# The last three attention units written out one by one, router columns cast later, eight zero products first

## The chip, the cores and the metric

The kernel runs on one core of one Trainium2 chip. The metric is the device time of one execution in microseconds. Its engines work side by side, each in the order of its own queue: TensorE (PE; its weight loads are PEld), VectorE (DVE), ScalarE (ACT), GpSimd (POOL) and SyncE (SP), which issues most DMAs.

## What is computed

A cross-attention layer and a mixture-of-experts layer, each with a layer norm ahead and a residual. Sizes: 32 sequences of 100 tokens (3,200 tokens), width 512, 16 heads of 32, 16 experts of 1,024 hidden units, all in float32.

```
q = (layernorm(x) @ WQ.T), k = ctx[:, :100] @ WK.T, v = ctx[:, :100] @ WV.T    # causal, so 100 keys are enough
x = x + softmax(mask(q k.T / sqrt(32))) v @ Wfc.T + bfc
h = layernorm(x)
shared = (gelu(h @ Ws_g.T) * (h @ Ws_u.T)) @ Ws_d.T
scores = softmax(h @ gate_w.T)              # over 16 experts
for each expert: its 12 best tokens of each sequence (384 tokens), gated MLP, times the score
out = x + shared + sum of the experts' parts, added back at the tokens' rows
```

The context has 722 rows for a sequence; the causal mask leaves the first 100.

## The kernel before

Each float32 operand of a large product is split into a high part (a cast on ACT, type fp32r) and a low part (a subtraction, source minus high part), and a product is three products, high by high, high by low, low by high (`mm3`, line 55). "A split" below is such a cast and subtraction.

**Attention** walks 32 units: eight blocks of four sequences (400 tokens) times four chunks of four heads. `prologue()` (L309) loads and splits the projection weights and the first context blocks, and computes the first keys and values. Keys and values go to DRAM (`kD`, `vD`) and come back by `kload` and `vload`. Then the loop over `u` works on three units at a time, in an order written out by hand:

- unit u: its query projection `qproj` on PE and `qkeep` on ACT; the key and value projections of a later context block, while there are any
- unit u-1: `scores` on PE into PSUM tile `sc` (one buffer of four banks); `sm_max` on DVE (16 small operations with the mask and the row maximum), `sm_sub` on POOL, `sm_exp` on ACT, `sm_sum` on DVE (sum and reciprocal), `sm_mul` on POOL, in two halves of two sequences
- unit u-2: `p_turn` (four transposes on PE into PSUM tile `ms`, two buffers), `p_keep` (copied out by ACT), `values` on PE (also into `ms`)
- unit u-3: `y_keep`, ACT's copy of the values, and their store to `yD`

Every engine's queue has exactly this order: PE, ACT, DVE and SP are under a manual schedule in the whole kernel, POOL in the attention. An instruction that waits holds everything behind it on its engine.

**Preparation of the first token group.** The FFN works on groups of two or three tiles of 128 tokens. For group 0 (three tiles) the loop's last three units also carry the steps of class `Prep`: `load_y`, `load_x`; `split_y(i)` (ACT and DVE), `bias(i)` (POOL, or DVE), `fc(i)` (twelve products on PE into `kv`, two buffers), `add(i)`, `stats(i)` (DVE), `rsqrt(i)` (POOL), `norm(i)` (DVE), `store(i)` (a DMA), `turn(i)` (four transposes on PE into `ms`, then a split), `logits` and `tokens` (the router's columns). In the loop they hang on `end`, which is 0, 1, 2 in units 29, 30, 31. After the loop follows a tail for unit 31's softmax and values, within which `F.begin` issues the first `gate_up_mm` of the FFN on PE and `F.begun` its gelu.

**Weight chunks.** The shared expert's and the experts' weights come as chunks of 128 x 1536 (eight to an expert, 768 KB). `chunk_load` issues the DMA of the next chunk into one of two raw buffers; `chunk_split(n, part)` splits it, whole or a third at a time, and then asks for the next load, which waits until the raw buffer is free.

**Router columns.** `load_consts` (L571), called in unit 13, issues three loads (bias, row bases, router weights `gr`), clears `gw` on POOL, and splits `gr` into `gw` at once (L577 on ACT, L578 on DVE).

The order inside unit 31 (`end == 2`) before, as an example, with the lines of other cases left out:

```
                if end == 2:
                    pr.add(2)
                    pr.stats(2)
                    pr.rsqrt(1)
                    pr.store(0)
...
                if end == 2:
                    pr.norm(1)
```

## Time and profile before

| | |
|---|---|
| median of 3 runs | 1696.91 us (1696.52 to 1699.1) |
| the profiled execution's own time | 1700.42 us |
| its span, first to last instruction | 1698.3 us |
| mean granted TensorE clock | 0.991 |
| attention with the preparation | 0 to about 389 us of the span |
| busy: PE, PEld, DVE, ACT, POOL | 98%, 90%, 55%, 41%, 36% |

Every line of a timeline has the start in us, the duration in us, engine, source line, operation, output <- input, and in brackets the time for which the engine was idle just before it and what released it. In a list of waits the numbers are the total, the number of waits and the longest. "Granted clock" is the share of TensorE's full clock in that stretch. Idle time of an engine costs something only where PE ends up waiting for it.

### The profile page before, as it was taken

What the parts mean: (1) busy time and instruction counts of PE and PEld (TensorE: products, weight loads), DVE (VectorE), ACT (ScalarE), POOL (GpSimd) and SP (SyncE); (2) the same over time, 40 slices, a digit from 0 to 9 for tenths busy, and PEclk for the clock granted to TensorE, in tenths of its full rate; (3) what the DMA queues carried; (4) which work ended last, traced back from release to release, by engine and by line L of the source; (5) the groups of instructions that cost most, each with busy time, mean ns of one, the idle gap of its engine ahead of it and who ended that gap; (6) DMA issues with size and microseconds to landing.
All of it is one profiled execution on the core that took longest, in us unless ns stands there. A gap on an engine that the chain in (4) does not pass through costs nothing.

```text
span 1698.3 us, 27985 instructions
## 1 busy us (share of the span) xinstructions
PE 1668.4 (98%) x10838; PEld 1533.6 (90%) x10838; DVE 929.2 (55%) x2191; ACT 691.0 (41%) x1097; POOL 619.5 (36%) x534
## 2 busy tenths in 40 slices
PE   7999999989999999999999999999999999999999
PEld 6998899879999999989899999999999999999998
DVE  4777677685434344344555555555555555555542
ACT  4555555543222112122334444444444444444442
POOL 3877777661110111110143443433444333344011
PEclk9999999999999999999999999999999999999999
DMA  6445444434322123210445554555554555555452
GB/s 211 151 141 160 134 135 121 160 113 143 104 75 70 52 71 97 82 57 27 147 153 160 156 163 152 147 160 160 166 159 145 162 150 152 163 168 152 133 168 63
DMA packets 97892, 224.35 MB, mean 132 GB/s; under 512 B 13633, under 2 KB 49186, under 8 KB 97760
## 3 DMA queue, kind: packets, MB, share of 16 engines
q1 hardware_dynamic: 84528, 197.08, 35.7%
q0 software_dynamic: 12944, 25.22, 7.9%
q8 instruction: 85, 1.39, 0.3%
q14 instruction: 47, 0.39, 0.1%
q10 hardware_dynamic: 288, 0.27, 0.0%
HBM read 175.34 MB, written 47.18 MB: 131 GB/s over the span
## 4 chain that ended last, share of the span: by engine, by line
PE 93%; DVE 2%; ACT 1%; POOL 1%; DMA 1%; issue 1%; SPq 0%; ACTq 0%; POOLq 0%; DVEq 0%
PE gu L55 48%; PE dn L55 24%; PE kv L55 11%; PE m L55 3%; PE ms L280 2%; PE sc L239 2%; PE ms L295 2%; POOL p L259 1%; DVE p L250 1%; PE m L989 1%; ACT pt L285 1%; PE ms L170 0%; DMA kD<-kk 0%; DMA big<-yD 0%; ACT p L263 0%
## 5 line engine op out<-in xcount | busy, mean ns | idle before, releaser
L55 PE MATMUL gu<-xh,whl 128*128 128x384 f32 (+1 forms) x3200 | 645.4, 333 | 0.0
L55 PEld LDWEIGHTS gu<-xh,whl 128*128 128x128 f32 x3200 | 560.6, 188 | 17.2 <-issue 0.3
L638 DVE TENSOR_TENSOR whl<-wraw,whl 128x1536 fp32r<-128x1536 f32 (+1 forms) x146 | 256.6, 1758 | 206.3 <-ACT whl L637 184.7
L55 PE MATMUL dn<-whl,hh 128*128 128x512 f32 x1168 | 368.0, 396 | 0.0
L840 POOL DMA_INDIRECT gx<-xnD,iq x180 | 226.7, 1259 | 362.2 <-DVE big L871 301.9
L55 PE MATMUL gu<-xl,whl 128*128 128x384 f32 (+1 forms) x1600 | 337.8, 332 | 0.0
L55 PEld LDWEIGHTS gu<-xl,whl 128*128 128x128 f32 x1600 | 280.7, 188 | 0.0
L673 ACT CAST hh<-g 128x384 fp32r<-128x384 f32 (+1 forms) x200 | 100.9, 505 | 409.0 <-DVE g L670 380.6
L55 PEld LDWEIGHTS dn<-whl,hh 128*128 128x128 f32 x1168 | 215.8, 188 | 37.0
L670 DVE TENSOR_TENSOR g<-g,gu 128x384 f32<-128x384 f32 (+1 forms) x200 | 108.3, 542 | 241.6 <-PE gu L55 237.0
L637 ACT CAST whl<-wraw 128x1536 fp32r<-128x1536 f32 (+1 forms) x146 | 213.0, 1459 | 64.1 <-PE dn L55 61.0
L55 PE MATMUL dn<-whl,hl 128*128 128x512 f32 x584 | 230.6, 395 | 0.0
L669 ACT ACTIVATE g<-gu 128x384 f32<-128x384 f32 (+1 forms) x200 | 96.2, 481 | 234.8 <-PE gu L55 234.1
L674 DVE TENSOR_TENSOR hl<-g,hh 128x384 fp32r<-128x384 f32 (+1 forms) x200 | 111.8, 559 | 114.2 <-ACT hh L673 113.8
L882 POOL DMA_INDIRECT out_dram<-x,isl x48 | 77.7, 1619 | 172.9 <-ACT x L881 163.2
L55 PEld LDWEIGHTS dn<-whl,hl 128*128 128x128 f32 x584 | 109.8, 188 | 26.2
L259 POOL TENSOR_TENSOR p<-p,mx 100x800 f32<-100x800 f32 x64 | 96.5, 1527 | 72.9 <-DVE mx L250 69.7
L274 POOL TENSOR_TENSOR p<-p,sm 100x800 f32<-100x800 f32 x64 | 103.1, 1613 | 10.6 <-DVE sm L269 9.8
L250 DVE CUSTOM_DVE_ANT_0 p<-sc,mask 100x100 f32<-100x100 f32 x512 | 95.7, 257 | 12.1 <-PE sc L239 11.5
L926 POOL TENSOR_TENSOR x<-x,bfc 128x512 f32<-128x512 f32 x22 | 29.9, 1383 | 170.5 <-DMA x<-x 170.0
L872 ACT CAST xh<-big 128x512 fp32r<-128x512 f32 x59 | 36.7, 622 | 100.2 <-DVE big L871 100.2
L268 DVE TENSOR_REDUCE sm<-p 100x8 f32<-100x800 f32 x64 | 63.0, 985 | 21.9 <-ACT p L263 21.8
(152 smaller groups left out, 1650.7 us busy)
## 6 DMA issues: line engine op xcount, KB each, us to landing
wraw<-wE SPq DMA_DIRECT2D x144, 768.0 KB
xt<-x SPq DMA_DIRECT2D x32, 200.0 KB
vD<-vt SPq DMA_DIRECT2D x25, 256.0 KB
kt<-kD SPq DMA_DIRECT2D x32, 200.0 KB
v<-vD SPq DMA_DIRECT2D x8, 800.0 KB
xnD<-xn SPq DMA_DIRECT2D x25, 256.0 KB
out_dram<-x SPq DMA_DIRECT2D x25, 256.0 KB
yD<-y SPq DMA_DIRECT2D x31, 200.0 KB
```

The costliest lines, as they stand in the source:

```text
L55: r = nc.tensor.matmul(out, t[0][a], t[1][b], start=(first and i == 0), stop=(last and i == n - 1))
L250: nc.vector.tensor_tensor_reduce(out=p[:, bb, h, :], in0=sc[:, h, cs], in1=mask, scale=ISCALE, scalar=NEG, op0=ALU.add, op1=ALU.max, accum ...
L259: nc.gpsimd.tensor_tensor(pv, pv, mx[:, :, None].to_broadcast([S, 8, S]), ALU.subtract)
L274: nc.gpsimd.tensor_tensor(pv, pv, sm[:, :, None].to_broadcast([S, 8, S]), ALU.mult)
L637: nc.scalar.copy(h[:, cs], r[:, cs])
L638: nc.vector.tensor_tensor(l[:, cs], r[:, cs], f32(h[:, cs]), ALU.subtract)
L669: nc.scalar.activation(g[:, 0:t], pg[:, 0:t], AF.Gelu)
L670: nc.vector.tensor_tensor(g[:, 0:t], g[:, 0:t], pu[:, 0:t], ALU.mult)
L673: nc.scalar.copy(hh[:, 0:t], g[:, 0:t])
L674: nc.vector.tensor_tensor(hl[:, 0:t], g[:, 0:t], f32(hh[:, 0:t]), ALU.subtract)
L840: nc.gpsimd.indirect_dma_start(out=g[:, k, :], out_offset=None, in_=self.K.xn.rearrange("t (a f) -> (t a) f", f=128), in_offset=bass.Indir ...
L882: ins = nc.gpsimd.indirect_dma_start(out=self.K.out, out_offset=bass.IndirectOffsetOnAxis(ap=r.isl[:, i:i + 1], axis=0), in_=o, in_offset= ...
```

## The change

It has three parts.

1. The general loop runs over units 0 to 28. Units 29, 30 and 31 and the tail are written out, step by step, in `last_units`. The steps are the same; their order on every engine's queue is new. The subtractions of weight chunks 0 and 1 (in six thirds) go to POOL, where before DVE did them (chunk 1 in one piece); `bias(2)` goes from DVE to POOL; the weight loads, key loads, stores and the load of the next group's y stand at other places of SP's queue; fc(1) and fc(2) no longer share a unit; `logits` comes after the first `gate_up_mm`.
2. The split of the router columns leaves `load_consts` and becomes `split_consts`, called in unit 15, ahead of its `scores`. The three loads and the memset stay in unit 13.
3. `prologue` begins, behind the mask's load, with a cleared 128 x 128 tile and eight float32 products of it with itself, into an `ms` buffer that nobody reads.

```diff
+WARM = 8
...
         def prologue():
             nc.gpsimd.dma_start(mask, K.mask)
+            z = stp.tile([128, 128], F32, name="zero")
+            nc.vector.memset(z, 0.0)
+            zp = ps_ms.tile([128, NC4, 128], F32, name="ms")
+            for _ in range(WARM):
+                nc.tensor.matmul(zp[:, 0, :], z, z, start=True, stop=True)
...
+        def turns(u, *bs):
+            for b in bs:
+                p_turn(u, b)
+
+        def keeps(u, *bs):
+            for b in bs:
+                p_keep(u, b)
+
+        def softmax_in(u):
+            scores(u)
+            y_keep(u - 2)
+            for hb in range(2):
+                sm_max(u, hb)
+                sm_sub(u, hb)
+
+        def last_units(pr):
+
+            gp = nc.gpsimd
+            u = NU - 3
+            kload(u)
+            F.chunk_load()
+            softmax_in(u - 1)
+            qkeep(u, qproj(u))
+            vload(nsb - 1)
+            turns(u - 2, 0, 1)
+            keeps(u - 2, 0, 1)
+            turns(u - 2, 2, 3)
+            sm_exp(u - 1, 0)
+            sm_sum(u - 1, 0)
+            sm_mul(u - 1, 0)
+            pr.split_y(0)
+            sm_exp(u - 1, 1)
+            sm_sum(u - 1, 1)
+            sm_mul(u - 1, 1)
+            keeps(u - 2, 2, 3)
+            pr.bias(0)
+            pr.split_y(1)
+            pr.fc(0)
+            pr.split_y(2)
+            values(u - 2)
+            kload(u + 1)
+            F.chunk_load()
+            pr.bias(1)
+            pr.add(0)
+            F.chunk_split(0, 0, gp)
+
+            u = NU - 2
+            softmax_in(u - 1)
+            pr.stats(0)
+            pr.rsqrt(0)
+            qkeep(u, qproj(u))
+            turns(u - 2, 0, 1)
+            sm_exp(u - 1, 0)
+            keeps(u - 2, 0, 1)
+            sm_sum(u - 1, 0)
+            sm_mul(u - 1, 0)
+            sm_exp(u - 1, 1)
+            pr.fc(1)
+            sm_sum(u - 1, 1)
+            sm_mul(u - 1, 1)
+            turns(u - 2, 2, 3)
+            keeps(u - 2, 2, 3)
+            pr.norm(0)
+            pr.bias(2)
+            kload(u + 1)
+            pr.store(0)
+            pr.add(1)
+            values(u - 2)
+            F.chunk_split(0, 1, gp)
+
+            u = NU - 1
+            softmax_in(u - 1)
+            pr.stats(1)
+            pr.rsqrt(1)
+            qkeep(u, qproj(u))
+            turns(u - 2, 0, 1)
+            keeps(u - 2, 0, 1)
+            sm_exp(u - 1, 0)
+            pr.fc(2)
+            sm_sum(u - 1, 0)
+            sm_mul(u - 1, 0)
+            sm_exp(u - 1, 1)
+            pr.norm(1)
+            turns(u - 2, 2, 3)
+            keeps(u - 2, 2, 3)
+            sm_sum(u - 1, 1)
+            sm_mul(u - 1, 1)
+            pr.store(1)
+            pr.turn(0)
+            values(u - 2)
+            pr.turn(1)
+            pr.add(2)
+            pr.stats(2)
+            pr.rsqrt(2)
+            F.chunk_split(0, 2, gp)
+
+            softmax_in(u)
+            F.ask(1)
+            turns(u - 1, 0, 1)
+            pr.norm(2)
+            keeps(u - 1, 0, 1)
+            turns(u - 1, 2, 3)
+            keeps(u - 1, 2, 3)
+            sm_exp(u, 0)
+            values(u - 1)
+            pr.turn(2)
+            sm_sum(u, 0)
+            sm_mul(u, 0)
+            y_keep(u - 1)
+            sm_exp(u, 1)
+            pr.store(2)
+            scctx.close()
+            F.open_gu()
+            F.begin(pr.done())
+            sm_sum(u, 1)
+            sm_mul(u, 1)
+            for i in range(3):
+                F.chunk_split(1, i, gp)
+            turns(u, 0, 1)
+            keeps(u, 0, 1)
+            pr.logits()
+            turns(u, 2, 3)
+            keeps(u, 2, 3)
+            F.begun()
+            values(u)
+            pr.tokens()
+            y_keep(u)
...
+                if u == FC_AT + NC4 + 2:
+                    F.split_consts()
...
+            last_units(pr)
...
         nc.gpsimd.memset(f32(gw), 0.0)
+
+    def split_consts(self):
+        nc, gw, gr = self.nc, self.gw, self.gr
         nc.scalar.copy(gw[:, :, 0:NE], gr)
         nc.vector.tensor_tensor(gw[:, :, 32:32 + NE], gr, f32(gw[:, :, 0:NE]), ALU.subtract)
...
-    def chunk_split(self, n, part=None):
+    def chunk_split(self, n, part=None, eng=None):
         nc, f = self.nc, n % NFC
         if n not in self.sw:
             hl = self.wp[f].tile([128, 2, 3 * D], FR, name=f"whl{f}")
@@ -635,7 +694,7 @@
         r = self.raws[n]
         cs = slice(0, 3 * D) if part is None else slice(part * D, (part + 1) * D)
         nc.scalar.copy(h[:, cs], r[:, cs])
-        nc.vector.tensor_tensor(l[:, cs], r[:, cs], f32(h[:, cs]), ALU.subtract)
+        (eng or nc.vector).tensor_tensor(l[:, cs], r[:, cs], f32(h[:, cs]), ALU.subtract)
         if part in (None, 2):
             self.chunk_load()
```

The removed lines are the `end` cases of the loop and the old tail, which stand in the kernel above.

## The prediction

> **What bounds the kernel now.** I read the page first, then the table of stages, then PE's waits, then each wait's place in the timeline.
>
> ```profile
> PE 1668.4 (98%) x10838; PEld 1533.6 (90%) x10838; DVE 929.2 (55%) x2191; ACT 691.0 (41%) x1097; POOL 619.5 (36%) x534
> 150.00:200.00 50.00, 46.77 (x515) 41.50 (x513) 32.96 (x166) 26.22 (x55) 36.09 (x32) 0.93 0.42 130
> 350.00:400.00 50.00, 43.77 (x388) 38.22 (x388) 32.85 (x101) 24.32 (x41) 20.84 (x16) 0.86 0.34 117
> 400.00:440.00 40.00, 40.00 (x219) 36.94 (x218) 21.38 (x30) 12.65 (x20) 1.58 (x4) 1.00 0.38 125
> ```
>
> The columns of a stage are its length, then PE, PEld, DVE, ACT and POOL busy, the granted clock and DMA. TensorE is the bound. From 400 us on it neither waits nor slows, so what is won or lost before 400 arrives whole at the end. The change can act only where the clock stands below 1: around 165 us, from 334 to 389, and in the first 23.
>
> ```profile
> PE kv L55 <- ACT cxh L134: 5.0, 1, 5.0
> PE ms L280 <- ACT pt L285: 4.0, 4, 2.4
> PE kv L55 <- ACT kk L203: 3.9, 1, 3.9
> PE ms L860 <- ACT pt L285: 3.5, 2, 3.2
> PE ms L280 <- ACT y L302: 2.3, 1, 2.3
> PE ms L280 <- POOL p L274: 1.4, 1, 1.4
> ```
>
> These waits (total, times, longest) are few, but each costs more than its length: while PE waits its clock falls to half.
>
> **1. Router columns.** Unit 13 starts at 161.79 with `scores`, unit 14 at 178.65.
>
> ```profile
> 161.79 0.96 PE L239 MATMUL sc<-kt,q 32*100 32x100 f32 x32
> 167.08 0.24 ACT L577 CAST gw<-gr 128x64 fp32r<-128x64 f32 x1 [4.45 <-DMA gr<-gwT]
> 167.77 0.55 PE L280 MATMUL ms<-ident,p 100*100 100x100 f32 x4 [2.29 <-ACT y L302]
> 169.94 1.48 PE L55 MATMUL kv<-cxh,wl 128*128 128x384 f32 x4
> 178.65 0.96 PE L239 MATMUL sc<-kt,q 32*100 32x100 f32 x32
> ```
>
> ACT stands 4.45 us at the cast; behind it in its queue is `y_keep`, which frees the PSUM buffer that the fourth transpose needs. PE loses 2.29 us, then 0.62, and four products take 1.48 instead of 0.86. Units with the same work start at 300.20, 310.96 and 321.70: 10.75 each. 16.86 − 10.75 = 6.1 us lost. The load was issued at 163.16 and landed by 167.08, so two units (21 us) later the cast finds it. The cast (0.24) and the subtraction (0.22) then stand ahead of a `sm_max` that begins about 1 us after `scores` anyway: nothing, and 0.5 if that cover failed. SP's three loads and POOL's memset stay put. I take −6.1; ends −6.4 and −5.5.
>
> **2. Eight zero products.** From 5.03 to 8.73 seventeen products stand 0.213 apart; warm ones stand 0.12 apart: 1.6 us.
>
> ```profile
> 16.77 0.37 ACT L203 COPY kk<-kv 128x256 f32<-128x256 f32 x1 [2.75 <-DMA kD<-kk]
> 17.19 0.79 PE L55 MATMUL kv<-wh,cxh 128*128 128x512 f32 x1 [3.87 <-ACT kk L203]
> ```
>
> PE ends this work at 13.3 and waits until 17.19 for ACT, which waits for a key write to land. That write is issued at 8.94, behind a raw load held until 8.36 by the split that empties its buffer; DMA is 0.8 to 1.1 busy in nearly every 2 us up to 22 us. An earlier kproj starts the write 0.14 us earlier at most. The Trainium skill ("TensorE: Matmul & The Clock Gate", Part 1) says that about 3.4 us of matmul activity releases the clock; by that alone the sum would have −1.6. By the row it has 0: the gain ends in the wait, which also makes the clock cold again (0.50 from 16 to 22 us). The price is bounded by L239: each f32 product of `scores` makes two records of 0.25 us, so sixteen in a row end 4 us after about 1.0 (DVE, which clears their operand, is idle there), before 5.03; if cold doubles that, they end at 9, and the 3.87 us wait swallows about all of it. I take 0; ends −0.2 and +1.0.
>
> **3. The last units.** Between 330.03 and the end of the second `gate_up` (389.13) PE needs, by rows at full clock: scores 4 × 0.90, qproj 3 × 2.29, ten pairs of turns × 0.63, fc 3 × 2.87, values 5 × 0.83, three `turn` × 0.68, logits 1.46, two gate_ups × 4.24, tokens 0.28: 41.8 us. It takes 59.1, so 17.3 us can be won at most. They are lost in four places, one line each, and the last line is a slice at half clock:
>
> ```profile
> 336.46 1.54 PE L280 MATMUL ms<-ident,p 100*100 100x100 f32 x8 [2.40 <-ACT pt L285]
> 349.69 1.95 DVE L638 TENSOR_TENSOR whl<-wraw,whl 128x512 fp32r<-128x512 f32 x1
> 360.83 1.13 PE L860 MATMUL ms<-ident,xn 128*128 128x128 f32 x4 [3.22 <-ACT pt L285]
> 379.90 0.89 PE L280 MATMUL ms<-ident,p 100*100 100x100 f32 x8 [1.40 <-POOL p L274]
> 384.00:386.00 2.00, 2.00 (x8) 2.00 (x8) 0.56 (x1) 1.59 (x3) 0.00 (x0) 0.50 0.22 81
> ```
>
> I walk the new order queue by queue, in the time of before. Durations: exp 0.88 (next start 0.78), keep 0.49 (0.38), cast 0.62 (0.52); a `sm_max` half 1.46, `sm_sum` 1.2, stats 0.9; on POOL `sm_sub` 1.5, `sm_mul` 1.5, bias 1.3, rsqrt 0.8. The six weight subtractions move from DVE (1.44 to 1.95 here) to POOL, where the trace has them only through L101 of the same shape: 1.29. Ends 1.0 and 2.9 (the slowest POOL row here, a `sm_mul` beside a DVE subtraction); I take 1.3.
>
> Unit 29. Keeps 0 and 1 now come ahead of the exps, so turns 2 and 3 go at 334.35 and not 336.46. fc(0) starts when its first y part is cast, 336.0; values end at 339.8 (342.45 before): −2.6.
> Unit 30. On POOL, `sm_mul` ends at 340.3, bias(0), bias(1) and the first subtraction at 344.4. Only then comes `sm_sub` (to 345.9 and 347.4), 1.6 us later after `scores` than usual; DVE's `add` also waits for bias(0). ACT waits in exp, with both keeps behind it, so PE waits 0.8 ahead of turns 2 and 3 and 1.2 ahead of values, which end at 350.0 (353.56): −3.5, though with one fc fewer (2.9).
> Unit 31. POOL reaches `sm_sub` at 353.8 (after mul 351.2, bias(2), subtraction). fc(2), now here, covers most; waits of 0.8 ahead of turn(0) and turn(1). End 361.1 (366.44): −5.3.
> Tail. DVE's `sm_max` of unit 31 starts only at 364.0, behind turn(1), add(2) and stats(2). norm(2) follows at 367, turn(2) on PE at 367.9, gate_up(0) at 369.3. Before that PE has waited about 4.5 of 8 us. Warm it would end at 373.6, cold at 376. Then turns, logits, turns to 378.7, values 380.5, tokens, second gate_up to 385.0, where before has 389.13: −4.1. The first `down` and fc behind it wait for ACT's chain (table load 1.28, gelu, cast, chunk 2, y split): fc ends at 388.2 against 391.93. I take −3.7.
>
> SP's reordered issues: weight load 1 goes behind key load 30, and load 2 waits for POOL's subtraction at 366.2 with y writes, the store of xn(2) and the next y load behind it. Their readers come after 380 and the loads land in about 5 us: nothing; if it failed, the wait is 1 to 2 us.
>
> Here a rule speaks against the trace. The same skill page ("Why this matters for your kernels") puts the fall of the clock at idle gaps above about 3 us. By it, my walk (longest wait 1.8) stays warm and part 3 is −6. By the rows, 1.40 us at 379.90 with 0.29 behind it halved the clock from 381 to 387, and three gaps in my tail are like it. So the cold gate_up stays in the sum. Ends for part 3: −8.8 (half of the 17.3) and +1.5 (two more cold spells, near 336 and 348, at about 2.3 us each, and a POOL that is 0.6 us later).
>
> Sum: −6.1 + 0 − 3.7 = −9.8 us. The profiled execution has a span of 1698.3 and 1700.42 as its own time, 3.5 above the median of 1696.91; 1700.4 − 9.8 = 1690.6 on that, 1687.1 against the median.
>
> **The rivals.**
> A. As above: 1687. Chance 0.53.
> B. POOL takes over. It is busy 32.9 of the 59.1 us before and gets about 8 more; if its waits and two more cold spells eat part 3, only the router is left: 1696.9 − 6.1 = 1690.8, with a little lost 1692. For it: `sm_sub` late in units 30 and 31. Against: PE's largest waits sit behind exps and keeps that the order does move. Chance 0.22.
> C. The clock holds through the tail and POOL keeps pace: part 3 is −6 to −8.8, 1682 to 1685. Chance 0.18.
> D. Slower. The bare mechanism is POOL's queue: from 336.7 to 374 it has about 32 us of work in one order, with PE's turns behind every op. To be 3.4 us slower it must be 13.2 us later than my walk: 0.41 of that work, a mean op of 2.1 instead of 1.5. It decides if most ops cost like the 2.87 row; at that price (+0.9) 1696.9 − 9.8 + 29 = 1716, at the deciding point 1700.3. Against: nine of ten `sm_mul` took under 1.8. Chance 0.02.
> E. The change doesn't do what it says: the cast waits again at unit 15 (another load late) and the tail only moves its waits: within 3 us of before. The landing at 167 speaks against it. Chance 0.05.
>
> **How the numbers follow.** 0.2% (3.4 us) is about what a measurement of this kernel tells from no change. A, B and C are faster by more: 0.93. E is 0.05, D 0.02. Likeliest 1687.1. The range adds the ends: −6.4 − 0.2 − 8.8 = −15.4 and −5.5 + 1.0 + 1.5 = −3.0; both at once are unlikely, so 1681.7 to 1692.9, which leaves out D, E and the rim of C.
>
> **What would show it.** Unit 13 at 10.7 us, no wait at L577. First key products at 0.12 spacing but PE again waiting until about 17 us. Turns 2 and 3 of unit 29 near 1 us after the first two; `sm_sub` of units 30 and 31 right behind POOL subtractions; the clock at 0.5 around the first gate_up. Wrong if that gate_up is warm, or PE starts its third key block well before 17.

## The result and the profile after

The changed kernel takes 1693.93 us (median of 20 runs, 1692.28 to 1696.22). The kernel before, measured beside it, takes 1697.43 us (20 runs, 1696.03 to 1701.13). The ratio is 0.9977, 95% interval 0.9971 to 0.9984: 3.9 us faster by the ratio, 3.5 by the medians. That is above the forecast range of 1681.7 to 1692.9, and about two fifths of the forecast gain of 9.8.

The profiled execution took 1693.86 us, with a span of 1692.1. That is close to its median, while the profiled execution of before lay 3.0 above its own. First the page's line for TensorE, then the stages, with the same columns as before (length, PE, PEld, DVE, ACT, POOL, granted clock, DMA share, GB/s).

```profile
PE 1664.7 (98%) x10854; PEld 1530.1 (90%) x10854; DVE 924.6 (55%) x2187; ACT 691.2 (41%) x1099; POOL 627.4 (37%) x541
```

```profile
150.00:200.00 50.00, 48.95 (x573) 44.08 (x572) 37.12 (x201) 27.92 (x59) 38.38 (x34) 1.00 0.51 151
...
350.00:400.00 50.00, 43.58 (x350) 38.26 (x350) 26.38 (x76) 24.35 (x40) 22.69 (x21) 0.97 0.36 123
400.00:440.00 40.00, 40.00 (x226) 36.87 (x225) 21.85 (x31) 13.05 (x20) 1.82 (x3) 1.00 0.45 145
```

The stage of the router columns is healed: the clock is 1.00 instead of 0.93, and PE is busy 48.95 us instead of 46.77. The stage of the last units is not: PE is still idle for 6.4 of 50 us there (6.2 before). PE's waits (total, times, longest) show why:

```profile
PE kv L56 <- ACT kk L204: 4.4, 3, 3.5
PE ms L296 <- ACT pt L286: 3.9, 10, 0.6
PE ms L281 <- ACT pt L286: 3.0, 4, 1.5
PE ms L919 <- DVE xn L1015: 2.2, 1, 2.2
```

The wait of 2.29 us for `y` is gone, and so is the 3.22 at `turn(0)`; the zero products now fill most of the 5.0 us at the start. The wait for the key write at the start remains, and in the last units there are many short waits and a new one of 2.2 us for `xn`.

Two measures are used from here on. "Unit 13" is the time from the first `scores` product of one loop turn to that of the next, in the turn in which the router constants are loaded. "The stretch" runs from the first `scores` product of unit 29 to the first `down` product (`dn`), and falls into unit 29, unit 30, unit 31 and the tail. All entries are us from one trace each.

| kernel | unit 13 | unit 29 | unit 30 | unit 31 | tail | stretch |
|---|---|---|---|---|---|---|
| before | 16.86 | 12.42 | 11.11 | 12.88 | 25.49 | 61.90 |
| before again (aa) | 15.25 | 12.34 | 11.11 | 12.59 | 24.83 | 60.87 |
| router part alone (r_only) | 11.75 | 12.20 | 11.11 | 12.60 | 24.98 | 60.89 |
| after | 11.75 | 9.80 | 11.47 | 12.22 | 27.16 | 60.65 |
| new order alone (t_only) | 15.46 | 9.80 | 12.12 | 11.55 | 28.54 | 62.01 |

The new order wins 2.6 us in unit 29 and gives most or all of it back in unit 30 and, above all, in the tail. The old order has other traces below with the same work in these units; its stretch lies between 60.79 and 61.90 in all seven, so neither 60.65 nor 62.01 shows a difference of the whole. What was left to settle was which part brings the 3.9 us, and what takes the gain of unit 29 away.

### The profile page after: what moved, and what is told of

Same layout as the page of the kernel before. It is cut to its first block, busy times and chain, and to the rows that moved or that the text cites. A ratio compares the mean times of both kernels' runs of the same rounds, so it can differ in the third digit from the quotient of the medians.

```text
span 1692.1 us, 28026 instructions
## 1 busy us (share of the span) xinstructions
PE 1664.7 (98%) x10854; PEld 1530.1 (90%) x10854; DVE 924.6 (55%) x2187; ACT 691.2 (41%) x1099; POOL 627.4 (37%) x541
## 4 chain that ended last, share of the span: by engine, by line
PE 93%; DVE 2%; ACT 2%; DMA 1%; POOL 1%; issue 1%; SPq 0%; ACTq 0%; POOLq 0%; DVEq 0%
PE gu L56 48%; PE dn L56 24%; PE kv L56 11%; PE m L56 3%; PE ms L281 2%; PE sc L240 2%; PE ms L296 1%; DVE p L251 1%; POOL p L260 1%; ACT pt L286 1%; PE m L1048 1%; PE ms L171 0%; DMA kD<-kk 0%; DMA yD<-y 0%; ACT p L264 0%
## 5 line engine op out<-in xcount | busy, mean ns | idle before, releaser
L697 DVE TENSOR_TENSOR whl<-wraw,whl 128x1536 fp32r<-128x1536 f32 x142 | 249.8, 1759 | 205.8 <-ACT whl L696 184.3
```

Of the source, the lines that this page charges most:

```text
L697: (eng or nc.vector).tensor_tensor(l[:, cs], r[:, cs], f32(h[:, cs]), ALU.subtract)
```

## Experiments

### The three parts, each alone, and the kernel before again

`r_only` is before with the later router cast:

```diff
+                if u == FC_AT + NC4 + 2:
+                    F.split_consts()
...
+    def split_consts(self):
...
```

> The kernel before with part 1 alone: the router columns are cast in unit 15, nothing else. Theory (the three parts add up, and the router cast is nearly all of the gain): the period from the scores of unit 13 to the next falls from 16.9 us to 11.8 as in the changed kernel's trace, not to 10.75, since the FC weight subtraction on DVE (1.48 us) still makes the row maxima late; median 3 to 5 us faster. Rival (the stall costs less in most executions[...]): 1.5 to 3 us. Rival (the lost time comes back later): 0.

Measured: 1694.03 us (11 runs), ratio 0.9978 (0.9969 to 0.9987). Unit 13 took 11.75 us, as in after.

`w_only` is before with the zero products alone:

```diff
...
+            for _ in range(WARM):
+                nc.tensor.matmul(zp[:, 0, :], z, z, start=True, stop=True)
```

> The kernel before with the eight zero products alone. Theory: 0 within 0.5 us, because PE then only waits longer for ACT's copy of the third key block, which waits for the first key write to land at about 17 us. Rival (warm clock carries on): 1.6 us faster. Rival (the products delay the first key products): up to 0.5 us slower.

Measured: 1697.67 us (13 runs), ratio 0.9998 (0.9990 to 1.0006).

`t_only` is before with the new order alone:

```diff
-            for u in range(NU):
+            for u in range(NU - 3):
...
+            last_units(pr)
```

> The kernel before with the last units written out in the new order alone; the router cast stays in unit 13. Theory: from the scores at the start of unit 29 to the end of the first fc of the second group 60.7 us against 61.9 before, so about 1 us faster, and within 1.5 us of no change in the median; on DVE one subtraction of the second y part takes over 4 us beside POOL. Rival (my recorded sum): 3.7 us faster. Rival (the new order is slower in the median, the profiled execution of before being an unlucky one): 1 to 2 us slower.

Measured: 1697.9 us (13 runs), ratio 0.9997 (0.9989 to 1.0006).

`aa` is before, unchanged.

> The kernel before once more, unchanged, for a second trace and for the spread. Theory: median within 1 us of before; the trace has the same waits of PE, but other stretches at half clock in the first 390 us, so its span differs by 1 to 3 us from 1698.3. Rival: the stretches at half clock are the same.

Measured: 1697.61 us (13 runs), ratio 0.9999 (0.9991 to 1.0007).

What follows: the router part carries the whole measured gain (0.9978 alone, 0.9977 together). The other two are worth nothing within about 1 to 2 us each way. `aa` has a second use, as a second trace of before. The stages of 4 us inside unit 13, first of before, then of `aa`:

```profile
168.00:172.00 4.00, 3.42 (x16) 2.91 (x14) 3.64 (x31) 1.38 (x4) 2.82 (x2) 0.64 0.15 53
172.00:176.00 4.00, 3.96 (x14) 3.41 (x15) 2.43 (x5) 2.71 (x6) 3.90 (x5) 0.50 0.35 77
```

```profile
168.00:172.00 4.00, 3.91 (x16) 3.40 (x15) 3.64 (x28) 1.57 (x4) 3.13 (x3) 0.57 0.14 53
172.00:176.00 4.00, 4.00 (x36) 3.28 (x37) 2.13 (x5) 2.92 (x8) 3.90 (x5) 1.00 0.35 91
```

The clock (the third figure from the right) is 0.50 from 172 to 176 in the profiled execution of before, and 1.00 in `aa`; the first four value products, which fall into this stage, took 2.06 us in the one and 1.18 in the other. The traces of `w_only`, `t_only`, `aa` and `kkx`, which all cast the router columns in unit 13, give 15.25, 15.46, 15.25 and 15.41 us. The 16.86 that the forecast read was the exception. In `w_only` the clock did not fall in unit 13 at all, and the unit still took 15.25 us: PE's second wait was 1.61 us there, against 0.62 in before. So it is the waits that cost these 4.6 us; the first spell at half clock cost nothing here, and the second the other 1.6.

### Which engine does the extra work

`bias_dve` and `sub_dve` are after with one kind of operation moved from POOL back to DVE.

```diff
-            pr.bias(0)
+            pr.bias(0, nc.vector)
...
-            pr.bias(1)
+            pr.bias(1, nc.vector)
```

> The changed kernel with the bias additions of tiles 0 and 1 in unit 29 on DVE instead of POOL. Theory (the second y part's subtraction on DVE, 4.5 us in the changed kernel, is starved by POOL's back-to-back softmax and bias operations, and that makes unit 30 late): that subtraction falls to about 1 us, the row maxima of unit 29 start about 1 us after their scores instead of 4.5 us, the 1.46 us wait in unit 30 goes, and from the scores of unit 29 to the first down product 60.65 us becomes 57.5 to 59.5; median 1 to 3 us below the changed kernel. Rival (unit 30 is late because POOL has too much to do in any order): 60 us or more, the wait stays.

Measured: 1693.67 us (9 runs), ratio 0.998 (0.997 to 0.999), stretch 60.62. The two bias adds took 0.80 and 0.68 us on DVE, but a `y` subtraction still took 3.25 there, and the row maxima of unit 30 still began 4.5 us after `scores`.

```diff
-            gp = nc.gpsimd
+            gp = None
```

> The changed kernel with the six subtractions of weight chunks 0 and 1 on DVE, as before the change. Theory (they are not what holds unit 30; POOL's biases and softmax operations do that): the stretch from the scores of unit 29 to the first down product stays within 1 us of 60.65. Rival (POOL is the bound, as my recorded case B): 1.5 to 3 us shorter. Rival (on DVE beside POOL they cost 1.5 to 2 us each): 2 to 4 us longer.

Measured: 1694.05 us (8 runs), ratio 0.9974 (0.9963 to 0.9984), stretch 61.77, with a wait of 2.18 us in unit 30 where after has 1.46. What follows: it does not help to pass single operations from one of the two engines to the other. That is no proof yet that they get in each other's way.

### The clock alone

`fill` is after with zero products put on PE where it waits: five in unit 30, ahead of the late turns, and in the tail six ahead of `turn(2)` and two behind it, so that the clock stays up.

```diff
+        def fill(u, n):
+            z, sc = cur["z"], cur["sc", u]
+            for _ in range(n):
+                nc.tensor.matmul(sc[:, 0, 4 * S:D], z[:, 0:S], z[:, 0:D - 4 * S], start=True, stop=True)
```

> The changed kernel with zero products (five ahead of the late turns of unit 30, six ahead of turn(2) and two ahead of the first gate_up) in TensorE's waits, written to unused columns of the scores tile; no other work is changed. Theory (stretches at half clock after those waits cost about 1.5 us each): no slice below full clock between 340 and 375 us, stretch 60.65 us becomes 57.5 to 58.5, median 2 to 3 us below the changed kernel. Rival (the slow stretches lie beside waits for ACT and POOL, so that a full clock only lengthens the next wait): under 1 us.

Measured: 1692.94 us (8 runs), ratio 0.9971 (0.9961 to 0.9982), stretch 60.40. The clock stayed at 1.00 from 340 to 358 (after has 0.50 for 3.4 us there), but the waits of unit 31 grew to 1.05 and 1.47 us, and units 29 to 31 together took 33.58 us against 33.49 in after. In units 30 and 31 a faster PE only waits longer, so the half clock is not what limits them. In the tail the clock fell all the same, to 0.50 from 359 to 366, and the tail took 26.82 us against 27.16; for the tail `fill` decides nothing.

### The order on POOL and DVE

`order2` is after with the bias adds, one `y` split and the weight subtractions moved to places where POOL was idle in the trace: bias(0) behind the softmax subtractions of unit 29, `split_y(2)` and bias(1) behind `rsqrt(0)` in unit 30, the first two parts of chunk 0 behind the last `sm_mul` of unit 31. In the order of the code:

```diff
+            pr.bias(0)
...
-            pr.bias(0)
...
-            pr.split_y(2)
...
-            pr.bias(1)
...
-            F.chunk_split(0, 0, gp)
...
+            pr.split_y(2)
+            pr.bias(1)
...
-            F.chunk_split(0, 1, gp)
...
+            F.chunk_split(0, 0, gp)
...
+            F.chunk_split(0, 1, gp)
```

> The changed kernel with POOL's and DVE's queues put in another order and no work moved between engines: bias(0) behind the first softmax subtractions of unit 29, bias(1) and the last y part behind the row maxima and rsqrt of unit 30, the three subtractions of weight chunk 0 behind the softmax products of unit 31. Theory (unit 30 is late because the row maxima of unit 29 stand on DVE behind y subtractions that POOL starves and an add that waits for POOL's bias, and because POOL's softmax subtraction stands behind biases and a weight subtraction): the row maxima of unit 29 start within 2 us of their scores (4.5 in the changed kernel), the softmax subtraction within 4 us (6.2), PE's wait ahead of the late turns of unit 30 falls from 1.46 to under 0.5, and the stretch from the scores of unit 29 to the first down product is 57.5 to 59.5 instead of 60.65. Rival (the delay only moves to unit 31 or the tail): 60 us or more.

Measured: 1693.28 us (7 runs), ratio 0.997 (0.9958 to 0.9981), stretch 60.68. Unit 30 fell from 11.47 to 8.66 us, with its wait at 0.29. Unit 31 rose from 12.22 to 13.49, and the tail from 27.16 to 28.73, with the clock at half from 354 to 371. The timeline of `order2` in unit 31 (start, duration, engine, line, operation, idle time before it and who ended it):

```profile
342.78 3.00 POOL L275 TENSOR_TENSOR p<-p,sm 100x800 f32<-100x800 f32 x2
...
342.99 3.08 DVE L1015 TENSOR_SCALAR xn<-x,mv,rs 128x512 f32<-128x512 f32 x1
...
352.60 0.75 PE L919 MATMUL ms<-ident,xn 128*128 128x128 f32 x4 [1.85 <-ACT pt L286]
...
356.70 1.67 PE L240 MATMUL sc<-kt,q 32*100 32x100 f32 x32
```

`norm(0)` takes 0.50 us in after. Here it was issued 0.21 us behind the first of two POOL multiplications that follow each other without a gap, and ended 0.29 us after both: 3.08 us. Behind it on DVE stand add(1) and the row maxima. The lateness left unit 30 and came back in unit 31.

### The end of unit 31

`add2` is after with three steps of tile 2 ahead of `turn(0)`, so that DVE reaches the last row maxima earlier.

```diff
+            pr.add(2)
+            pr.stats(2)
+            pr.rsqrt(2)
             pr.turn(0)
             values(u - 2)
             pr.turn(1)
-            pr.add(2)
-            pr.stats(2)
-            pr.rsqrt(2)
```

> The changed kernel with add(2), stats(2) and rsqrt(2) ahead of turn(0) and turn(1) in unit 31. Theory (unit 31's row maxima start late because these stand behind turn(1)'s subtraction on DVE, and norm(2) and turn(2) behind them): row maxima begin about 1 us after the scores instead of 2.9, the 2.2 us wait ahead of turn(2) falls to about 0.5, the stretch is 1.5 to 2 us shorter. Rival (turn(0) and turn(1) become late by as much): no change.

Measured: 1693.31 us (21 runs, 1690.67 to 1696.45), ratio 0.9976 (0.9970 to 0.9983), while the traced execution has a stretch of only 58.84. In its timeline `turn(2)` no longer waits for `xn` (it stood 2.21 us in after):

```profile
363.56 0.90 PE L296 MATMUL ms<-pt,v 100*32 100x100 f32 x32 [0.29 <-ACT pt L286]
364.55 0.72 PE L919 MATMUL ms<-ident,xn 128*128 128x128 f32 x4
365.94 0.97 PE L56 MATMUL gu<-xh,whl 128*128 128x384 f32 x4 [0.68 <-ACT xh L920]
```

The first gate_up ran at full clock (0.97 us for four products, against 1.65 in after), and the tail took 23.58 us instead of 27.16. Unit 31 took 13.32 instead of 12.22. The 21 times do not lie around one value: six are between 1690.6 and 1691.7, nine between 1695.2 and 1696.5, and six lie between the two groups. The trace belongs to the first six, so the 1.8 us of its stretch are not a gain of the median.

### The start, and what the router part left

`kkx` is before with the third and fourth block of the first keys copied into value buffers that are idle then, so that ACT needs no finished key write to go on.

```diff
-            kk = kkp.tile([128, KMAX], F32, name="kk")
+            kk = (vtp.tile([128, D], F32, name="vt") if spare else
+                  kkp.tile([128, KMAX], F32, name="kk"))
...
-            kkeep(0, 2, p0)
+            kkeep(0, 2, p0, True)
```

> The kernel before with the third and fourth key blocks of the prologue copied into two value buffers that are idle then, so that these copies don't wait for a key write to land. Theory (that wait is what holds PE from 13 to 17 us): the 3.9 us wait falls below 1.5 us, the clock stays up, the first scores come 2 to 4 us earlier than 42, median 2 to 4 us faster than before. Rival (DMA bounds the start: the value weights land at about 17 us anyway): first scores within 1 us of 42, no change.

Measured: 1695.92 us (21 runs), ratio 0.9991 (0.9984 to 0.9998). That is 1.5 us by the ratio, less than the 2 to 4 that were expected. The first `scores` began at 40.24 us, but kernels without this edit have it anywhere from 40.48 (`r_only`) to 42.86 (`w_only`), so only the times show the gain. The wait of 3.87 us for `kk` became one of 1.40 for a weight load:

```profile
17.48 0.49 PE L55 MATMUL kv<-wh,cxh 128*128 128x512 f32 x1 [1.40 <-ACT wh L100]
```

`r_best` is before with the router cast, `kkx`, and the fourth of the `Wfc` splits moved from the end of unit 12 to the end of unit 13 (`FC_AT` is 9):

```diff
-                if FC_AT <= u < FC_AT + NC4:
+                if FC_AT <= u < FC_AT + 3:
                     F.fc_split(u - FC_AT, fr)
+                if u == FC_AT + NC4:
+                    F.fc_split(3, fr)
```

> The kernel before, old order in the last units, with three small edits: the router cast in unit 15, the fourth FC weight split in unit 13 instead of unit 12, and two key blocks of the prologue copied into idle value buffers. Theory: unit 13 takes 10.75 us instead of 11.75 (the FC split was the next thing late), first scores near 40.3; 3.7 + 1.0 + 1.6 = about 6 us below before. Rival (the FC split makes unit 14 late instead): 5 us.

Measured: 1690.74 us (5 runs), ratio 0.9957 (0.9943 to 0.9970). Unit 13 took 10.75 us, the value of an undisturbed unit; the stretch, in the old order, 61.41.

`combo2` is after with `order2`, `add2` and both of these edits.

> All that helped in the traces at once, on the changed kernel: the other order of POOL and DVE, add(2) ahead of turn(0), the fourth FC split in unit 13, two key blocks in value buffers. Theory: the gains add up: 6 us as in the kernel with three small edits, and 2 to 4 us in the last units; 8 to 10 us below before, the stretch from the scores of unit 29 to the first down product 56.5 to 58.5. Rival (the last units give their gain back as in the changed kernel): 6 us below before.

Measured: 1692.14 us (5 runs), ratio 0.9963 (0.9949 to 0.9976). Unit 30 took 8.67 us, unit 31 15.00, the clock was at half from 351 to 369, and the stretch was 61.08, where 56.5 to 58.5 had been expected. The reordered POOL queue loses again what it wins.

### Both orders without POOL's extra work

If DVE and POOL are in each other's way, the new order must show its gain once the extra operations are left out. `quiet_new` (from after) and `quiet_old` (from `r_only`) leave out the same six operations, the three bias adds and the three low-part subtractions of chunk 0 (the low part is cleared once instead), so their output is not the layer's. In the new order all six stand on POOL; in the old one two bias adds do, and the other four stand on DVE. The edit of `quiet_new` (`quiet_old` has the like at its own places):

```diff
-            pr.bias(0)
...
-            pr.bias(1)
...
-            pr.bias(2)
...
-        (eng or nc.vector).tensor_tensor(l[:, cs], r[:, cs], f32(h[:, cs]), ALU.subtract)
+        if n or part is None:
+            (eng or nc.vector).tensor_tensor(l[:, cs], r[:, cs], f32(h[:, cs]), ALU.subtract)
```

> The kernel after, with the three bias adds of the first token group and the three low-part subtractions of weight chunk 0 left out (the low part is cleared once ahead of unit 29), so that part of the computation is missing. Theory (POOL's extra work in units 29 to 31 and what it does to DVE eats the gain of the new order): the stretch from unit 29's first scores to the first down product falls from 60.7 to about 57, DVE's y subtractions take 0.7 to 1.1 us, row maxima begin about 1 us after scores in units 30 and 31, and the time is 3 to 4 us below quiet_old. Rival (the order itself is worth nothing: its waits only move): the stretch is within 1 us of quiet_old's, and the time within 1 us too.

> The kernel before with the router part alone, and with the same three bias adds and three low-part subtractions of chunk 0 left out and the low part cleared once (part of the computation is missing). Theory: the old order suffered less from these operations, so the stretch falls by 1 us at most from 61.2, to 60 to 61, and the time is that of the router part alone, 0.9978 of before, or 1 us less. Rival: the old order gains as much from their absence as the new one does, and both end alike.

`quiet_add2` is `quiet_new` with the edit of `add2`.

> quiet_new (bias adds of the first token group and low parts of chunk 0 left out, so part of the computation is missing) with add, stats and rsqrt of tile 2 ahead of turn 0. Theory: the two losses are separate, so the units keep quiet_new's 29.5 us and the tail takes add2's 23.6 instead of 28.3: a stretch near 54 us (53 to 55), 1685 to 1686 us. Rival: the tail's loss is the clock's alone and comes back at another wait, or add(2) ahead of turn 0 delays unit 31 as it did in add2 (13.3 against 12.2): 56 to 58 us, no better than 1688.

| kernel | us | ratio to before | units 29, 30, 31 | tail | stretch |
|---|---|---|---|---|---|
| quiet_old | 1690.68 | 0.9964 (0.9951 to 0.9978) | 12.56, 11.12, 10.74 | 23.92 | 58.34 |
| quiet_new | 1689.35 | 0.9953 (0.9939 to 0.9966) | 9.82, 8.95, 10.68 | 28.26 | 57.71 |
| quiet_add2 | 1686.67 | 0.9927 (0.9913 to 0.9941) | 9.80, 8.98, 11.37 | 23.96 | 54.11 |

The theory holds for the units: without these operations they take 29.45 us in the new order and 34.42 in the old, a gain of 5.0, and units 30 and 31 are 4.1 us shorter than in after. `quiet_new` missed its forecast as a whole, being 1.3 us below `quiet_old` by the medians and not 3 to 4, because the tail took 28.26 us, with the clock at half from about 357 to 367. The two intervals overlap, and the stretches lie 0.6 us apart, which is what the rival had said; so this pair alone does not show that the new order is worth anything as a whole. `quiet_add2` removes the loss in the tail too and meets the 54 us of its expectation; its interval lies clear of that of `quiet_old`. The old order also gained from the quiet (58.34 against about 61), which I had put at 1 us at most.

The timeline of `quiet_new` shows the relief. Its last two `y` subtractions stand beside the two multiplications of `sm_mul` and take 2.81 us together, where the same two take 5.30 in after:

```profile
330.13 3.93 POOL L275 TENSOR_TENSOR p<-p,sm 100x800 f32<-100x800 f32 x2 [1.11 <-ACT p L264]
331.80 2.81 DVE L976 TENSOR_TENSOR yl<-big,yh 128x512 fp32r<-128x512 f32 x2
334.53 0.68 DVE L995 TENSOR_TENSOR x<-kv,x 128x512 f32<-128x512 f32 x1
```

### The best version

`combo3` is after with `add2`, the key blocks in spare buffers and the moved fourth `Wfc` split, without `order2`. `r_best2` is `r_best` again, measured beside it, `combo3_2` is `combo3` again.

> The kernel after, with add, stats and rsqrt of tile 2 ahead of turn 0 (as add2), the fourth FC weight split in unit 17 (two units after the others' last one), and the two prologue key blocks in spare value buffers. Theory, adding the stretches: 58.8 in the last units against 61.2 of the old order, unit 13 at 10.75, so 2 us below r_best2, near 1688.7 (0.9945 of before). Rival: the last units' gain shows in one trace only and not in the times: within 0.7 us of r_best2.

(The "unit 17" in this text is a slip for unit 13, one unit after the others' last one.)

> The same kernel as r_best, again, as the measure for combo3 in the same call: 0.9957 of before as it was, within 0.0008.

> combo3 again, with more runs. If its tail is steady, all runs lie within 1687 to 1691 with a ratio near 0.9946. If it has the two groups that the runs of add2 show (1691 and 1696 there), some runs lie 4 us above the others, at about 1692, and the ratio rises to 0.995 to 0.996.

Measured: `combo3` 1688.65 us (5 runs, 1687.71 to 1689.83), ratio 0.9946 (0.9933 to 0.9960). `r_best2` beside it 1690.86 (1690.56 to 1693.63), ratio 0.9960 (0.9946 to 0.9973). `combo3_2` 1689.96 (1688.58 to 1695.11), ratio 0.9946 (0.9933 to 0.9960). `combo3` is the fastest kernel of this study that computes everything: 9.2 us below before by the ratio, 5.3 below after. Its interval overlaps that of `r_best2`, but of the runs that were measured side by side none was as slow as the fastest of the other.

Nine of the ten runs of `combo3` and `combo3_2` lie between 1687.7 and 1690.4, one at 1695.11, and that one is the traced execution of `combo3_2`. So here two traces of one program, 5 us apart, can be laid side by side. The stretch took 58.91 us in the one and 63.20 in the other. Both stand at the same wait in unit 30 (1.47, and 0.59 behind it); the timeline of PE, first of `combo3`, then of `combo3_2`:

```profile
341.58 0.87 PE L282 MATMUL ms<-ident,p 100*100 100x100 f32 x8 [1.47 <-ACT pt L287]
...
346.13 1.70 PE L56 MATMUL kv<-xnh,wh 128*128 128x400 f32 x4
```

```profile
342.55 0.86 PE L282 MATMUL ms<-ident,p 100*100 100x100 f32 x8 [1.47 <-ACT pt L287]
...
345.73 1.00 PE L56 MATMUL kv<-xnh,wh 128*128 128x400 f32 x4
```

In `combo3` the clock fell to half behind it (1.70 us for four products), in `combo3_2` it did not (1.00). The stages, in the same order:

```profile
339.49:342.90 3.41, 1.50 (x11) 0.88 (x9) 2.67 (x11) 2.71 (x6) 3.33 (x5) 1.00 0.13 47
342.90:349.73 6.83, 6.69 (x75) 6.19 (x76) 5.40 (x37) 1.49 (x4) 6.81 (x6) 0.50 0.19 71
...
366.00:368.00 2.00, 2.00 (x13) 2.00 (x12) 1.14 (x3) 0.94 (x2) 1.78 (x2) 1.00 0.80 298
```

```profile
338.44:341.85 3.41, 2.64 (x12) 1.82 (x10) 3.24 (x30) 0.69 (x1) 2.32 (x3) 1.00 0.62 227
341.85:345.26 3.41, 2.12 (x56) 1.79 (x60) 2.81 (x6) 3.31 (x8) 3.30 (x5) 1.00 0.04 15
...
355.50:372.57 17.07, 13.85 (x105) 12.03 (x106) 9.34 (x45) 7.53 (x14) 10.28 (x9) 0.50 0.41 133
```

These stages begin and end where the clock can change. In all 20 traces every spell at half clock in the first 400 us lasts 3.41 us or 2, 3 or 5 times that, and within one trace the spells begin whole multiples of 3.41 us apart (21.41, 168.18, 335.44, 359.33 and 379.81 in `aa`). So the clock changes at fixed points 3.41 us apart, wherever these fall in the kernel. In `combo3` nearly the whole pair of waits lies between two of them, and PE is idle for 1.91 of 3.41 us; in `combo3_2` the point at 341.85 parts the pair, and the idle times are 0.77 and 1.29. That fits the difference. A bound of idle time that decides does not come out of the traces: 1.28 us was followed by half clock in `quiet_new` and `t_only`, while 1.80 us was not in `w_only`.

Where PE was fast in unit 31 (`combo3_2`), it ran into waits of 1.04 and 2.98 us at its end, and then the clock was at half from 355 to 372, through the last transposes and the gate_up, which PE alone limits. Where PE was slow in unit 31, those waits were 0.29 and 0.98, and the tail ran at full clock: 23.58 us against 27.73. Units 29 to 31 together took the same in both, 35.33 and 35.47 us. DVE beside POOL plays into it again. In `combo3_2` `norm(1)` began 0.05 us behind a POOL multiplication and took 1.75 us; in `combo3` it began 0.22 us ahead of it and took 0.50. The timelines of `combo3_2` and of `combo3`:

```profile
352.91 1.52 POOL L276 TENSOR_TENSOR p<-p,sm 100x800 f32<-100x800 f32 x1
...
352.96 1.75 DVE L1018 TENSOR_SCALAR xn<-x,mv,rs 128x512 f32<-128x512 f32 x1 [0.20 <-POOL rs L1011]
```

```profile
353.48 0.50 DVE L1018 TENSOR_SCALAR xn<-x,mv,rs 128x512 f32<-128x512 f32 x1
...
353.70 3.13 POOL L276 TENSOR_TENSOR p<-p,sm 100x800 f32<-100x800 f32 x2 [1.78 <-DVE sm L271]
```

That the two outer groups of `add2` are these two courses is likely (the same code there, the same 4 to 5 us), but only one of them was traced, and six of its runs lie between them.

## Why the prediction was right in two mechanisms and wrong in its sum

**Part 1, the router columns: forecast −6.1, measured −3.7** (`r_only`, by the ratio, between 2.2 and 5.3 faster). The mechanism was right. The cast no longer waits, and `r_only` shows that this is the whole gain. Two terms of the sum were mis-sized.

The first is "16.86 − 10.75 = 6.1 us lost". Four other traces of the same code give 15.25 to 15.46, mean 15.34, so the usual loss is 4.6; the other 1.5 us was a second spell at half clock in the one execution that was profiled. The forecast noticed that this execution was 3.5 us above its median and still subtracted the whole loss from the median. A stall that is only in the slow execution cannot be won from the median. Nor does each wait cost more than its length because the clock falls, as the forecast set out from: `w_only` kept its full clock here and lost the same 4.5 us as `aa`.

The second is that unit 13 would become an undisturbed 10.75. It became 11.75. The timeline of after in unit 13:

```profile
161.68 0.96 PE L240 MATMUL sc<-kt,q 32*100 32x100 f32 x32
162.16 1.48 DVE L642 TENSOR_TENSOR wfl<-raw,wfh 128x512 fp32r<-128x512 f32 x1 [0.45 <-ACT wfh L641]
...
167.28 0.87 ACT L264 ACTIVATE p<-p 100x800 f32<-100x800 f32 x1 [1.72 <-POOL p L260]
...
168.58 0.95 PE L281 MATMUL ms<-ident,p 100*100 100x100 f32 x8 [0.73 <-ACT pt L286]
...
173.43 0.96 PE L240 MATMUL sc<-kt,q 32*100 32x100 f32 x32
```

Next late is the `Wfc` subtraction, 1.48 us on DVE beside a POOL multiplication, which holds the row maxima back. POOL's softmax subtraction comes late, ACT waits 1.72 us for it in the exponential, and PE waits 0.73 for ACT's copies. `r_best`, which moves that subtraction, has 10.75. So 15.34 − 11.75 = 3.6 is what the cast could win, and the times agree.

**Part 2, the zero products: forecast 0, measured 0** (`w_only`, 0.9998). The steps held as described. The timeline of after:

```profile
1.08 3.79 PE L316 MATMUL ms<-zero 128*128 128x128 f32 x16 [1.08 <-DVE zero L313]
...
17.23 0.37 ACT L204 COPY kk<-kv 128x256 f32<-128x256 f32 x1 [3.33 <-DMA kD<-kk]
...
17.65 0.50 PE L56 MATMUL kv<-wh,cxh 128*128 128x512 f32 x1 [3.48 <-ACT kk L204]
```

Eight float32 products made sixteen records and ended at 4.87, where the forecast had about 5. The first key products then stood 0.12 us apart (0.213 before), but for gaps of up to 0.53 in which they waited for their operands, and PE waited until 17.65 for the same key write. The rule weighed here (the Trainium skill, "TensorE: Matmul & The Clock Gate", Part 1) is not contradicted, since the key products did run warm; but the 1.6 us that the forecast derived from it end in the wait, as the row said.

**Part 3, the last units: forecast −3.7, measured 0** (`t_only`, 0.9997, between 1.9 us faster and 1.0 slower). The walk was right through unit 29: the forecast had −2.6 us, and the traces show 12.42 becoming 9.80. The step that failed is `sm_sub` in unit 30. The walk lets it go at 344.4, that is 4.6 us after the unit's `scores` (339.8), as soon as POOL is through bias(0), bias(1) and the first subtraction, and the sign it named was `sm_sub` right behind POOL's subtraction. In unit 31 that came true, in unit 30 not. The timeline of after:

```profile
331.75 3.94 POOL L275 TENSOR_TENSOR p<-p,sm 100x800 f32<-100x800 f32 x2 [1.09 <-ACT p L264]
334.23 4.50 DVE L975 TENSOR_TENSOR yl<-big,yh 128x512 fp32r<-128x512 f32 x1
...
335.64 2.53 POOL L985 TENSOR_TENSOR x<-x,bfc 128x512 f32<-128x512 f32 x2
338.13 1.72 POOL L697 TENSOR_TENSOR whl<-wraw,whl 128x512 fp32r<-128x512 f32 x1
338.65 0.68 DVE L994 TENSOR_TENSOR x<-kv,x 128x512 f32<-128x512 f32 x1
339.25 0.24 DVE L251 CUSTOM_DVE_ANT_0 p<-sc,mask 100x100 f32<-100x100 f32 x1
...
340.94 3.01 POOL L260 TENSOR_TENSOR p<-p,mx 100x800 f32<-100x800 f32 x2 [1.09 <-DVE mx L251]
342.50 0.87 ACT L264 ACTIVATE p<-p 100x800 f32<-100x800 f32 x1 [3.92 <-POOL p L260]
343.90 0.86 PE L281 MATMUL ms<-ident,p 100*100 100x100 f32 x8 [1.46 <-ACT pt L286]
```

`sm_sub` went at 340.94, 6.2 us after `scores` (334.71), and POOL had stood idle for 1.09 us ahead of it, waiting for DVE's row maxima. The walk has no term for a DVE operation that stands behind POOL, and that is what came: the last `y` subtraction took 4.50 us. It began while POOL was in `sm_mul`, and POOL went on to two bias adds and a weight subtraction without a gap; DVE was done at 338.73, just after the weight subtraction had begun, which in its turn took 1.72 us instead of the 1.28 that it takes elsewhere. Only then come add(0) and the row maxima, at 339.25 or 4.5 us after `scores`, POOL's `sm_sub`, ACT's exponential after 3.92 us of waiting, and PE.

In the walk units 30 and 31 take 10.2 and 11.1 us. They took 11.47 and 12.22 in after, 12.12 and 11.55 in `t_only`: 2.4 us more in both. The tail was priced at 27.1 us. It took 27.16 in after and 28.54 in `t_only`, with the same order, so the close hit in after is partly luck. The cold gate_up that the forecast kept in the sum did come, behind waits of 2.21 and 0.68 us (in full clock `add2` has 0.97 for the same four products):

```profile
365.47 0.72 PE L919 MATMUL ms<-ident,xn 128*128 128x128 f32 x4 [2.21 <-DVE xn L1015]
366.87 1.65 PE L56 MATMUL gu<-xh,whl 128*128 128x384 f32 x4 [0.68 <-ACT xh L920]
```

And the stretch of 61.90 from which the walk subtracts is the longest of the seven of the old order (median 61.16). The 2.4 us in the units, some 0.7 of start value and up to 1.4 in the tail account for the 3.7. What the walk didn't see is that the loss in the tail could be avoided: `add2` and `quiet_add2` show tails of 23.6 and 24.0.

The Trainium skill has the rule that the forecast should have weighed here. "SBUF — State Buffer", section "Who interferes with whom", says that a VectorE instruction with two SBUF inputs and a GpSimd instruction that reads SBUF contend for a shared port, that one in a two-port mode contends with GpSimd too, and that whichever issues first has the port for its whole length while the other is fully blocked. The rows agree. Two-input subtractions and the `norm` were hit (0.69 with POOL idle to 4.50, 0.50 to 3.08); the add at 338.65 and the row maxima, one input of which comes from PSUM, kept their length beside POOL.

The traces also tell a slowed operation from one that stands still. In the first 395 us of all 20 traces, DVE began 142 subtractions of the splits (`yl`, `whl`, `wfl`) while POOL was in an instruction. One of them began together with POOL's instruction and kept its length; the other 141 ended 0.54 to 0.55 us behind the end of a POOL instruction, whatever their own length. All 51 `norm` that began so ended 0.28 to 0.29 behind one. They show one thing more: where POOL's queue leaves no gap, DVE may stand through several POOL instructions, not one. It could have been read before: the `whl` subtraction of 1.95 us at 349.69, which the forecast shows, ends 0.54 us behind this one.

```profile
349.39 1.71 POOL L274 TENSOR_TENSOR p<-p,sm 100x800 f32<-100x800 f32 x1
```

`quiet_new` and `quiet_old` bear this out in the units: without the extra operations the new order wins 5.0 us by the end of unit 31. The 5.3 that the walk had there was no hit, since the walk had these operations in it. With the tail's loss away too, the new order wins 4.2 us of stretch (54.11 against 58.34), 4.0 by the medians and 6.3 by the ratios to the before beside each. The forecast's 3.7 is close to that by luck: it was for a kernel that does all the work and has the tail's loss.

**The rivals.** B, "POOL takes over, only the router left", is what happened. Its time of 1690.8 to 1692 was too low only because it took over the router's 6.1. Not POOL's own length was the cause, though, since its bias adds and weight subtractions took about what was forecast and it stood idle ahead of the late `sm_sub`, but DVE behind POOL. C had the clock as the decider; `fill` shows that a held clock alone wins nothing in the units. For D the forecast read nine of ten `sm_mul` below 1.8 us; of the ten of before from 328 us on it is eight, and the other two (1.97 and 2.87) had stood behind a DVE subtraction. The worst ends of the three parts add up to 1693.9, just about what was measured, but by luck: the parts were −3.7, 0 and 0, not −5.5, +1.0 and +1.5.

**What stays open.** When DVE gets in between two POOL operations was not settled: `norm(0)` at 346.09 in after got in behind the first of two multiplications and took 0.50 us, while in `order2` it stood through both and took 3.08. Nor is it settled how much idle time between two of the clock's points makes the clock fall. Whether any order of all the work gets near the 54 us of `quiet_add2` was not tried beyond `order2`, `combo2` and `combo3`.

## What to carry to other kernels

Read a stall in a second trace of the same program before you count it: what only the one execution lost is not to be won, and the unit that you repair stops at the next late thing, not at the length of an undisturbed one. When work moves to GpSimd, look at which two-input VectorE instructions stand beside it and price them by the whole unbroken run of GpSimd operations, then ask who is queued behind them. A wait or a half clock costs only where TensorE is the limit: here the same clock loss was free in one unit and cost 4 us in the next stage.

## What the runs showed of the hardware that I had not expected

- An operation on DVE beside POOL is not slowed a little but may stand for the whole of POOL's run: 0.69 to 4.50 us for a two-input subtraction, 0.50 to 1.75 and 3.08 us for `norm`, which reads one tile. Its end follows the end of a POOL instruction by 0.55 or 0.28 us. A start 0.05 us behind POOL was enough for the 1.75.
- The granted clock after the same two waits (1.47 and 0.59 us, the same instructions) was 0.50 in one execution of a kernel and 1.00 in another, and the executions ended 5 us apart. The clock changes only at points 3.41 us apart, and one of these points parted the waits in the second execution.
- The same stall in unit 13 was followed by 6.83 us at half clock in one trace of before, by 3.41 us in the other, and by none in `w_only`. The first unit took 16.86 us, the other two 15.25 each.
